# The end of a mixture-of-experts kernel: one branch instead of two, last sums of different banks declared independent, and idle products moved ahead of them

## The chip, the cores and the metric

The kernel runs on one core of a Trainium2 chip. The core has five engines that run side by side, each with its own queue of instructions: TensorE (PE: matrix products, and PEld: its weight loads), VectorE (DVE), ScalarE (ACT), GpSimd (POOL) and SyncE (SP, which here issues most of the transfers). [...] Time is device time in microseconds (us); lower is better. Three runs of the kernel before took 394.36, 396.98 and 397.94 us, median 396.98.

## What is computed

One transformer block on 16 sequences of 256 tokens of width 128, all in float32. It has causal attention with 16 heads of width 8, and eight experts of inner width 512, of which each token uses the two with the highest router logits. Layer norm comes after each half:

```python
def reference(x, w_qkv, w_proj, b_proj, W_router, b_router, W1, b1, W2, b2):
    x = _layernorm(x + attention(x, w_qkv, w_proj, b_proj))
    logits = x @ W_router + b_router
    top_vals, top_idx = jax.lax.top_k(logits, 2)
    weights = softmax over the two chosen logits
    y = sum over experts e of weights[:, e] * (relu(x @ W1[e] + b1[e]) @ W2[e] + b2[e])
    return _layernorm(x + y)
```

## The kernel before, in words

The program has a main path (`main_path`), which is quick and holds for ordinary data, and a plain `general_path` that recomputes everything. A flag, `spoiled`, says whether the main path met a softmax denominator outside a safe range; at the very end every engine loads that flag and skips the general path if it is zero (L1621, L1622).

The main path works in this order. Attention is done for one sequence ("batch") after the other. After batches 0 to 9, and again after 10 to 15, the tokens are routed: this makes two groups, group 0 of ten batches and group 1 of six. Tokens are scattered to DRAM, sorted by expert (`route`, L1046; `finish`, L1181, ends with the tables of block starts and a flag in `over` for more blocks than planned). Blocks of 128 or 256 rows of one expert are then fetched, put through both layers, and sent back to DRAM at the tokens' places (`block`, L1289). If a group had more blocks than planned, `leftover` (L1579) would do up to two more per group: it stands behind a first branch on the flag `any_over`, taken by every engine (L1580, L1581).

At the end of each group, `combine` (L1420) goes over its batches. For each batch: `fetch` (SyncE) loads the two experts' results of each token, tile `ys`; `add` sums them with the residual; `stats` (VectorE, `moments_of`, L742) takes mean and variance; `power` (GpSimd) raises the variance to −1/2; `shift` (VectorE) makes the offset; `scale` (ScalarE) writes the result to `yout`, of which there are three buffers; SyncE stores it.

In the last group `add` is done by TensorE, as products with the identity that accumulate in PSUM (L1465); `begin` (L1443) has put the residual there earlier. [...] Batches 0 to 3 of the last group use the four banks of one tile, `room`, a bank each; batches 4 and 5 have tiles of their own, of the kind "m", which has three buffers that go round. Because `room` is one tile, the framework that sets the semaphores makes an `add` into one bank wait for earlier reads of another bank of it.

`keep_warm` (L1538) makes twelve idle products whose result nobody reads. `check` (L1551) has `within` (VectorE: counts the good denominators), `total` (TensorE: one product that adds the counts over partitions), `missing` (VectorE: writes `spoiled`) and `exceeded` (VectorE: writes `any_over`).

The order of the work is written out: every step is registered as an operation with a number, a planner's cost and a rank, but `emit` only follows the list `ORDER` (L311). Costs, ranks and port flags of the operations are not read when the list is there. The list fixes each engine's own order; what waits for what between engines follows from the data. In it, five idle products stand while the last blocks run and seven after everything else. The last sums come in the order of batches 2, 4, 5, 3, 1, 0.

Of the kernel before, what the change touches and what calls it, by code (L numbers as in the profile page):

```python
# [22 lines left out]
HEADS = 16  # L23
# [318 lines left out]
499 782 610 611 612 530 531 932 933 892 500 783 784 980 981 645 1541 785 767 982 934 935 769  # L342
# [6 lines left out]
878 818 819 1227 848 891 820 1020 821 822 849 1021 1032 823 890 850 1018 877 939 824 1033 1542  # L349
1198 1034 949 1035 940 1543 1036 851 1494 1022 852 941 942 1023 948 1024 1235 950 968 951 943  # L350
1025 826 825 1231 944 969 1026 952 970 1229 1236 945 946 953 971 972 1037 1237 1048 1049 1205
954 973 906 955 1050 1051 1544 905 1201 956 974 975 1200 1027 907 908 976 947 1052 1053 909 911
1199 1088 910 912 1008 1054 913 1089 1090 914 959 915 1091 1055 957 977 960 958 961 1056 988
1092 1093 962 1094 963 1009 1095 1096 964 965 1210 1217 1216 966 989 1010 916 990 1011 1012
1057 918 917 919 991 801 802 1013 992 1097 853 1496 1014 1015 993 994 1219 1221 995 1016 920
921 922 967 996 923 803 998 854 1068 1069 1017 997 1222 804 805 807 806 808 924 925 926 855 856
809 999 810 811 858 1070 860 1078 857 1071 1079 859 1072 1073 861 1213 1212 927 1000 862 1074
1001 1002 863 1080 1211 1493 827 1075 1076 813 812 1003 828 1081 1082 1004 1005 1215 1038 1039
1083 829 830 1084 864 865 1085 1098 831 1006 1040 832 833 1041 1042 1077 834 1058 1043 1059 835
1060 1044 1061 1086 1099 836 1100 1062 1214 1007 1220 1045 1101 837 1102 1218 1063 1046 1251  # L360
1103 1064 1065 1087 1104 1393 1252 1253 1066 1105 1254 1255 839 838 1394 1047 1395 1256 1106
1257 1258 1483 1067 1264 1107 1484 1278 1277 1265 1172 1156 1396 1397 1398 1259 1260 1261 1485
1486 1399 1400 1401 1140 1279 1280 1173 1164 1487 1488 1282 1281 1263 1174 1262 1374 1284 1266
1373 1283 1267 1489 1175 1490 1402 1108 1141 1491 1353 1176 1177 1142 1132 1269 1354 1285 1286
1375 1376 1492 1268 1271 1178 1377 1143 1179 1287 1270 1144 1145 1378 1239 1157 1238 1158 1333
1146 1272 1289 1273 1159 1274 1288 1334 1355 1356 1160 1148 1363 1379 1240 1276 1357 1275 1343
1241 1380 1161 1133 1242 1381 1364 1358 1244 1243 1382 1290 1134 1135 1245 1162 1335 1336 1136
1344 1147 1359 1360 1361 1137 1149 1362 1291 1180 1337 1246 1338 1313 1247 1248 1250 1365 1366
1314 1249 1138 1150 1339 1340 1367 1345 1346 1347 1341 1342 1423 1163 1463 1368 1292 1151 1165
1293 1348 1166 1369 1370 1371 1167 1294 1296 1295 1372 1424 1297 1315 1316 1152 1153 1168 1169  # L370
1139 1349 1350 1464 1154 1124 1109 1323 1317 1318 1351 1324 1298 1299 1425 1170 1352 1300 1426
1413 1110 1319 1465 1466 1155 1320 1301 1427 1302 1111 1428 1321 1467 1414 1181 1325 1326 1429
1322 1468 1430 1431 1327 1433 1434 1469 1182 1432 1328 1470 1471 1415 1112 1329 1416 1417 1330
1435 1331 1418 1453 1183 1436 1437 1438 1472 1304 1419 1420 1421 1303 1454 1113 1332 1305 1473
1404 1403 1114 1439 1306 1440 1441 1422 1455 1307 1456 1457 1308 1474 1458 1442 1184 1185 1186
1405 1406 1309 1310 1407 1475 1408 1476 1459 1443 1444 1311 1384 1383 1312 1477 1460 1478 1461
1462 1445 1446 1409 1410 1411 1116 1412 1187 1447 1448 1385 1386 1479 1480 1387 1481 1449 1388
1125 1389 1450 1545 1546 1390 1482 1117 1451 1497 1118 1452 1391 1119 1115 1547 1392 1548 1126
1127 1128 1120 1129 1549 1121 1171 1498 1495 1513 1514 1515 1516 1122 1527 1528 1529 1130 1530
1517 1518 1534 1535 1536 1537 1520 1123 1506 1521 1531 1522 1532 1131 1538 1539 1507 1508 1523  # L380
1499 1500 1524 1501 1519 1533 1540 1509 1510 1525 1526 1511 1502 1503 1504 1512 1505 1550 1551
1552 1553 1554 1555 1556
# [72 lines left out]
def main_path(  # L455
# [64 lines left out]
    plans = [Plan()]  # L520
    plans[0].banks = {"sc", "ps_o", "m"}
    bufs = {p1: 1, p2: 2, p3: 3, p4: 4, p6: 6, p8: 8, ps_sc: 1, ps_o: 1, ps_m: 3}

    def op(*a, **kw):
        return plans[-1].op(*a, **kw)

    def tile_of(pool, tag, shape, dtype=F32):
        return plans[-1].tile(pool, shape, tag, bufs[pool], dtype)
# [61 lines left out]
    any_over = const.tile([1, 1], I32, name="any_over")  # L590
# [151 lines left out]
    def moments_of(mv, r):  # L742
        st = p4.tile([P, 6], F32, tag="st", name="st")
        V.bn_stats(st, r)  # L744
        V.bn_aggr(mv, st)

# [299 lines left out]
    def route(g, b, n):  # L1046
# [106 lines left out]
        chosen = op("DVE", 1.05, z, logits, after=[*x1_ops[b : b + n], br_op, table_op])  # L1153
        chosen = op("DVE", 1.15, z, choose, after=[chosen])
        chosen = op("DVE", 1.9, z, choose_next, after=[chosen])
        mats(z, 0.48, count, writes=[psc], after=[chosen])
        a = op("ACT", 0.12, z, weights_exp, after=[chosen])
        weighted = op("DVE", 0.6, z, weights, after=[a])
        g.placed = op("DVE", 1.8, z, totals, reads=[psc], after=counted)
        g.placed = op("DVE", 0.72, z, places, after=[g.placed])  # L1160
# [20 lines left out]
    def finish(g):  # L1181
# [90 lines left out]
        for k, n, fn, cost in ((1, g.ND, pairs, 1.65), (0, g.NB, singles, 1.6)):  # L1272
            experts, starts = of_each(n, str(k))
            go = op("DVE", cost, z, fn, after=[go])
            go = g.ready[k] = op("DVE", 0.45 + 0.015 * n, z, experts, after=[go])
            go = g.known[k] = op("DVE", 1.1 + 0.02 * n, z, starts, after=[go])
# [143 lines left out]
    def combine(g, sent):  # L1420
# [8 lines left out]
        acc, room = [], tile_of(ps_sc, "sc", [P, GROUPS, 2, S])  # L1429
        for b in range(g.n):  # L1430
            if not last:
                acc.append(tile_of(p2, "acc", [P, NT, D]))
            elif b < GROUPS:
                acc.append(tile_of(ps_sc, f"acc{b}", []))
                acc[b].get = lambda b=b: room.get()[:, b].rearrange(
                    "p a (o d) -> p (a o) d", d=D
                )[:, 0:NT, :]
            else:
                acc.append(tile_of(ps_m, "m", [P, NT, D]))

            def begin(b=b):
                rows = x1_sb[:, rows_of(b), 0:D]
                nc.tensor.matmul(  # L1443
                    acc[b].get(), ident, rows, start=True, stop=False, skip_group_check=True
                )

            if last:
                where, after = ([room], x1_ops) if b < GROUPS else ([], g.second)
                mats(z0 + 6.0 * b, 0.43, begin, writes=[*where, acc[b]], after=after, part="begin")

        for b in range(g.n):
# [9 lines left out]
            def add(b=b, ys=ys):  # L1461
                a = acc[b].get()
                if last:
                    for k in range(2):
                        nc.tensor.matmul(  # L1465
                            a,
                            ident,
                            ys.get()[:, :, k],
                            start=False,
                            stop=k == 1,  # L1470
                            skip_group_check=True,
                        )
                else:
# [3 lines left out]
            def stats(b=b, mv=mv):  # L1477
                for n in range(NT):
                    moments_of(mv.get()[:, n, :], acc[b].get()[:, n, :])
# [10 lines left out]
            def scale(b=b, rstd=rstd, off=off, yout=yout):  # L1490
                for n in range(NT):
                    nc.scalar.activation(
# [5 lines left out]
                    )  # L1498

            op("SP", 0.5, z, fetch, kb=256, writes=[ys], after=sent)  # L1500
            if last:
                mats(z, 0.88, add, reads=[ys], writes=[acc[b]])
# [35 lines left out]
    def keep_warm():  # L1538
        g = groups[-1]
# [7 lines left out]
        for i in range(WARM):  # L1547
            mats(2900.0, 0.43, turn_over, writes=[idle], after=g.second)


    def check():  # L1551
# [13 lines left out]
        def missing():  # L1565
            V.tensor_scalar(spoiled, psg.get(), -1.0, float(B * HEADS * S), ALU.mult, ALU.add)

        def exceeded():
            with nc.allow_low_precision(reason="0 or 1"):
                V.tensor_reduce(any_over, over, AX.X, ALU.max)  # L1570

        go = op("DVE", 2.6, z, within, writes=[good], after=dens_ops)
        mats(z, 0.2, total, writes=[psg], after=[go])
        op("DVE", 0.16, z, missing, reads=[psg])
        op("DVE", 0.16, 10.0 * B + 100.0, exceeded, after=found)

    def leftover():  # L1579
        some = nc.values_load(any_over[0:1, 0:1])  # L1580
        with tc.If(some > 0):  # L1581
            plans.append(Plan())
            for g in groups:
                sent = []
                for j in range(g.NB - SPARE, g.NB):
                    sent += block(g, j, 0)
                combine(g, sent)
            for o in plans[-1].ops:
                o["fn"]()
# [5 lines left out]
    b0, groups = 0, []  # L1595
    for r, chunks in enumerate(ROUTED):
# [9 lines left out]
        combine(g, sent)  # L1606
        groups.append(g)
    check()
    keep_warm()
    nc.scalar.preload_act_table_set("natural_log_exp_and_others")  # L1610
    with tc.manual_schedule():
        plans[0].emit()
    leftover()
# [68 lines left out]
```

## Time and profile before

The profile is of one execution that took 396.12 us by the device's own measure; from its first to its last instruction (the span) are 394.3 us.

| what | value |
|---|---|
| runs | 394.36, 396.98, 397.94 us; median 396.98 |
| profiled execution, span | 396.12 us, 394.3 us |
| mean granted TensorE clock | 0.962 |
| TensorE products / weight loads busy | 340.9 us (86%) / 250.5 us (64%) |
| VectorE, ScalarE, GpSimd busy | 212.5, 253.2, 218.7 us (54, 64, 55%) |
| from 0 to 370 us | attention, routing, experts, group 0's end |
| 370 to 387 us | group 1's end: products busy 11.63 us, statistics and scaling |
| 387 to 394.3 us | no engine is busy; branches and the end of the program |
| last sum (batch 0) | starts 382.53, on "sc" |
| last scaling (ScalarE) | ends 386.87 |
| last store | issued 386.89 |

How to read it. Engines are named as above; a name ending in q (DVEq, SPq) is the engine's sequencer, which does branches, flag loads and waits and is not counted as busy. "L1465" is a line of the kernel. In a group such as "sc<-ys,ident" the tile on the left is written from those on the right: "sc" is the tile `room`. An idle stretch is put down to what ended it, after "<-". The chain of waits is followed back from the last instruction of an engine; "issue" in it is time in which the engine waited for nothing that the profile shows. The windows view gives, for a stretch, its length, each engine's busy time, the granted clock of TensorE, the DMA engines' mean busy share and what they moved.

### The profile page before, as it was taken

Reading aid. Unit: us, or ns where it says so; the run is one execution under the profiler, and the core shown is the slowest. Engines: PE = TensorE matmul, PEld = TensorE weight load, DVE = VectorE, ACT = ScalarE, POOL = GpSimd, SP = SyncE. Lnnn points to the kernel's source line nnn. Section 1 sums busy time; section 2 is a strip of 40 time slices with the busy share of each in tenths; the row PEclk is TensorE's granted clock in tenths of the full one; section 3 lists DMA queues with packets and bytes.
Section 4 is the critical chain, followed back from the end, with each engine's and each line's share of the span. In section 5 each row is a group of like instructions: output and inputs, shape, how many; then the busy total and the mean of one; then the engine's idle time right before and its main releaser. Section 6 shows DMA issues by size and latency. Waiting matters only on the chain.

```text
span 394.3 us, 9755 instructions
## 1 busy us (share of the span) xinstructions
PE 340.9 (86%) x2960; PEld 250.5 (64%) x2960; DVE 212.5 (54%) x730; ACT 253.2 (64%) x547; POOL 218.7 (55%) x252
## 2 busy tenths in 40 slices
PE   5999999589986789759899899989899999999672
PEld 4555555256542455335479779878899898889651
DVE  3434457956778578794557872432222376633450
ACT  2788888368868277736645545555576688877522
POOL 5335434437886386867623367777776445454340
PEclk9999999979999699978999989999999999999988
DMA  5201322013241141343424635566755777766341
GB/s 134 17 4 45 95 76 56 23 52 91 73 129 30 37 115 58 83 120 89 134 62 140 159 123 142 154 191 173 209 155 163 240 226 226 212 190 191 110 148 51
DMA packets 53104, 46.57 MB, mean 118 GB/s; under 512 B 14610, under 2 KB 39577, under 8 KB 53042
## 3 DMA queue, kind: packets, MB, share of 16 engines
q1 hardware_dynamic: 48626, 37.36, 35.3%
q0 software_dynamic: 4416, 8.47, 6.4%
q8 instruction: 28, 0.46, 0.5%
q14 instruction: 34, 0.28, 0.2%
HBM read 33.53 MB, written 12.67 MB: 117 GB/s over the span
## 4 chain that ended last, share of the span: by engine, by line
PE 58%; DVE 18%; ACT 9%; DMA 8%; issue 4%; ACTq 0%; SPq 0%; DVEq 0%; POOLq 0%; POOL 0%
PE m L1337 14%; PE m L1358 14%; PE sc L869 9%; PE ps_o L910 8%; ACT pr L894 5%; PE m L791 5%; DMA spread<-recs 4%; PE m L964 2%; DVE key L1066 2%; DMA w<-in_L_ffn_W_dram 2%; DVE x_sb L994 1%; PE m L836 1%; DVE st L744 1%; PE sc L1465 1%; PE m L1321 1%
## 5 line engine op out<-in xcount | busy, mean ns | idle before, releaser
L1385 POOL DMA_INDIRECT back<-yw,rows_in x74 | 73.5, 993 | 62.8 <-ACT yw L1377 39.8
L894 ACT ACTIVATE pr<-sc 128x2048 f32<-128x2048 f32 x48 | 90.1, 1877 | 25.7 <-PE sc L869 25.0
L879 POOL TENSOR_SCALAR_AFFINE_SELECT pr<-pr 128x1024 f32<-128x1024 f32 (+1 forms) x48 | 68.5, 1435 | 65.0 <-ACT pr L894 60.4
L1350 ACT ACTIVATE hT<-m,b_sb 128x128 f32<-128x128 f32 (+1 forms) x224 | 72.1, 405 | 27.5 <-PE m L1337 19.1
L1337 PE MATMUL m<-rT,w 128*128 128x128 f32 (+1 forms) x448 | 75.9, 316 | 4.8 <-DVE rT L1330 3.0
L1138 POOL DMA_INDIRECT rows<-x_sb,dest x64 | 64.1, 1002 | 27.9 <-issue 17.1
L1358 PE MATMUL m<-w_sb,hT 128*128 x592 | 76.1, 278 | 2.4 <-ACT hT L1350 1.4
L1358 PEld LDWEIGHTS m<-w_sb,hT 128*128 128x128 f32 x592 | 71.3, 191 | 5.2 <-ACT hT L1350 3.6
L1337 PEld LDWEIGHTS m<-rT,w 128*128 128x128 f32 x448 | 62.3, 192 | 12.7 <-DVE rT L1330 5.2
L869 PE MATMUL sc<-qTm,qk 32*128 32x512 f32 x384 | 56.2, 655 | 7.9 <-ACT pr L894 7.2
L910 PE MATMUL ps_o<-pr,va 128*32 128x128 f32 (+1 forms) x1024 | 51.2, 342 | 0.5 <-ACT o L923 0.4
L1368 DVE TENSOR_TENSOR y<-m,b_sb 128x128 f32<-128x128 f32 (+1 forms) x56 | 18.7, 334 | 61.0 <-PE m L1358 39.3
L1377 ACT ACTIVATE yw<-y,rows_in 128x128 f32<-128x128 f32 x74 | 27.6, 400 | 30.0 <-DVE y L1368 27.5
L910 PEld LDWEIGHTS ps_o<-pr,va 128*32 128x32 f32 x1024 | 29.5, 115 | 22.5 <-issue 9.0
L820 ACT ACTIVATE qTm<-qk,rows_sb 128x256 f32<-128x256 f32 x64 | 29.8, 503 | 5.3 <-DVE qk L808 5.3
L869 PEld LDWEIGHTS sc<-qTm,qk 32*128 32x128 f32 x384 | 15.6, 190 | 21.7 <-ACT pr L894 18.1
L791 PE MATMUL m<-xT,wqk_sb 128*128 128x256 f32 x64 | 22.8, 440 | 5.3 <-ACT xT L781 5.3
L954 DVE TENSOR_TENSOR o<-o,spread 128x512 f32<-128x512 f32 x16 | 16.2, 1015 | 15.0 <-DMA spread<-recs 15.0
L791 PEld LDWEIGHTS m<-xT,wqk_sb 128*128 128x128 f32 x64 | 11.1, 206 | 19.6 <-ACT xT L781 8.1
L800 DVE TENSOR_TENSOR part<-m,rope_sb 128x256 f32<-128x256 f32 x32 | 13.2, 411 | 19.3 <-PE m L791 19.2
L964 PEld LDWEIGHTS m<-wproj_sb,o 128*128 128x128 f32 x128 | 16.1, 190 | 10.1 <-DVE o L954 4.5
L964 PE MATMUL m<-wproj_sb,o 128*128 128x136 f32 x128 | 18.5, 288 | 2.3 <-DVE o L954 2.1
(151 smaller groups left out, 377.7 us busy)
## 6 DMA issues: line engine op xcount, KB each, us to landing
w<-in_L_ffn_W_dram SPq DMA_DIRECT2D x56, 256.0 KB
spread<-recs SPq DMA_DIRECT2D x16, 256.0 KB
ys<-back SPq DMA_DIRECT2D x16, 256.0 KB
rows_in<-rows SPq DMA_DIRECT2D x38, 65.0 KB
rows_in<-rows SPq DMA_DIRECT2D x18, 130.0 KB
x<-in_L_attn_x_dram SPq DMA_DIRECT2D x16, 128.0 KB
w_sb<-in_L_ffn_W_dram SPq DMA_DIRECT2D x8, 256.0 KB
out_dram<-yout SPq DMA_DIRECT2D x16, 128.0 KB
```

The lines of the kernel that those rows point to most:

```text
L791: nc.tensor.matmul(ps.get()[:, c, :], w[:, s, :], xT.get(), start=True, stop=True)
L820: lambda j=j: nc.scalar.activation(qTm.get()[:, j, :], qk.get()[:, 0], AF.Copy, scale=rows_sb[:, j : j + 1]),
L869: nc.tensor.matmul(ps.get()[:, g], qk.get()[rg, 1, ts(kt, P)], qTm.get()[rg, js, kt * P : S], start=True, stop=True,)
L879: nc.gpsimd.affine_select(out=pr.get()[:, :, :, 0:P], in_=pr.get()[:, :, :, 0:P], compare_op=ALU.is_ge, fill=0.0, base=0, pattern=[[0, GRO ...
L894: lambda pr=pr, ps=ps: nc.scalar.activation(pr.get(), ps.get(), AF.Exp),
L910: nc.tensor.matmul(pso.get()[ts(g, 32), t, kt * P : S], va_t[:, kt, 2 * g + t].rearrange("p u c -> p (u c)")[:, 16 * u : 16 * u + 32], pr. ...
L964: nc.tensor.matmul(ps_p.get()[:, q, :], o.get()[:, t, ts(q, P)], wproj_sb[:, t, :], start=(t == 0), stop=(t == 1),)
L1138: nc.gpsimd.indirect_dma_start(out=g.rows[:, :], out_offset=bass.IndirectOffsetOnAxis(ap=g.dest[:, k, t - g.t0 : t - g.t0 + 1], axis=0), i ...
L1337: nc.tensor.matmul(ps_h[i].get()[:, c, :], w.get()[:, ts(i * per + c, P)], rT.get()[:, 0 : n * P], start=True, stop=True,)
L1350: nc.scalar.activation(hT.get()[:, at, 0 : n * P], ps_h[i].get()[:, c, :], AF.Relu, bias=bias)
L1358: nc.tensor.matmul(ps_y.get()[:, i, :], hT.get()[:, c, i * P : (i + 1) * P], w2_sb[:, bass.ds(e, 1), c, :].rearrange("p o d -> p (o d)"), ...
L1385: put = nc.gpsimd.indirect_dma_start(out=g.back[:, :], out_offset=bass.IndirectOffsetOnAxis(ap=rows_in.get()[:, i, D : D + 1].bitcast(I32) ...
```

## The change

Four things are done.

1. **One branch.** `leftover` and its branch go. `missing` now adds "a group had more blocks than planned" to the flag `spoiled`, so that one branch at the end serves both cases: such data go to the general path. `exceeded` goes as an operation of its own; the three small steps are one operation.
2. **The check is moved** in the order: `total` and `missing` stood apart in the expert stage of group 0, `exceeded` later; now `total` and `missing` stand directly behind the last operation of `finish` of group 1.
3. **Independence.** A helper `apart` collects the instructions that touch the banks of `room` in the last `combine`, and declares any two of them that are on different engines and on different banks free of a dependency.
4. **Idle products.** `keep_warm` is registered ahead of the last `combine`, its products are prerequisites of the sums, and in the order the seven that stood at the very end now stand between `begin` of batch 2 and the sum of batch 2.

Beside that the fetches of the last group stand earlier in the list, all before the first sum. Each engine's own order, SyncE's transfers included, is otherwise as before. The operations' numbers change, since the idle products are registered earlier and one operation less exists; so nearly all lines of `ORDER` differ, and they are left out here.

```diff
-    any_over = const.tile([1, 1], I32, name="any_over")
+    any_over = const.tile([1, 1], F32, name="any_over")
+    lost = const.tile([1, 1], F32, name="lost")
...
     def moments_of(mv, r):
         st = p4.tile([P, 6], F32, tag="st", name="st")
-        V.bn_stats(st, r)
+        read = V.bn_stats(st, r)
         V.bn_aggr(mv, st)
+        return read
...
-    def combine(g, sent):
+    def combine(g, sent, warm=()):
...
+        used_by = []
+
+        def apart(b, engine, put):
+            if last and b < GROUPS:
+                for other, by, i in used_by:
+                    if other != b and by != engine:
+                        tc.declare_no_dep(put.ins, i.ins, reason="another bank")
+                used_by.append((b, engine, put))
...
-                nc.tensor.matmul(
+                put = nc.tensor.matmul(
                     acc[b].get(), ident, rows, start=True, stop=False, skip_group_check=True
                 )
+                apart(b, PE, put)
...
-                        nc.tensor.matmul(
+                        put = nc.tensor.matmul(
                             a,
                             ident,
                             ys.get()[:, :, k],
...
+                        apart(b, PE, put)
...
-                    moments_of(mv.get()[:, n, :], acc[b].get()[:, n, :])
+                    apart(b, DVE, moments_of(mv.get()[:, n, :], acc[b].get()[:, n, :]))
...
-                    nc.scalar.activation(
+                    read = nc.scalar.activation(
                         yout.get()[:, n, :],
...
+                    apart(b, ACT, read)
...
-                mats(z, 0.88, add, reads=[ys], writes=[acc[b]])
+                mats(z, 0.88, add, reads=[ys], writes=[acc[b]], after=warm)
...
-        for i in range(WARM):
-            mats(2900.0, 0.43, turn_over, writes=[idle], after=g.second)
+        return [mats(2900.0, 0.43, turn_over, writes=[idle], after=g.second) for _ in range(WARM)]
...
         def missing():
-            V.tensor_scalar(spoiled, psg.get(), -1.0, float(B * HEADS * S), ALU.mult, ALU.add)
-
-        def exceeded():
-            with nc.allow_low_precision(reason="0 or 1"):
-                V.tensor_reduce(any_over, over, AX.X, ALU.max)
+            V.tensor_scalar(lost, psg.get(), -1.0, float(B * HEADS * S), ALU.mult, ALU.add)
+            V.tensor_reduce(any_over, over, AX.X, ALU.max)
+            V.tensor_tensor(spoiled, lost, any_over, ALU.add)
...
-        mats(z, 0.2, total, writes=[psg], after=[go])
-        op("DVE", 0.16, z, missing, reads=[psg])
-        op("DVE", 0.16, 10.0 * B + 100.0, exceeded, after=found)
-
-    def leftover():
-        some = nc.values_load(any_over[0:1, 0:1])
-        with tc.If(some > 0):
...
+        mats(z, 0.2, total, writes=[psg], after=[go, *found])
+        op("DVE", 0.55, z, missing, reads=[psg], after=found, port=True)
...
-        combine(g, sent)
-        groups.append(g)
+        combine(g, sent, keep_warm(g) if g.r == len(ROUTED) - 1 else [])
     check()
-    keep_warm()
     nc.scalar.preload_act_table_set("natural_log_exp_and_others")
     with tc.manual_schedule():
-        plans[0].emit()
-    leftover()
+        plan.emit()
```

The planner's costs and port flags of the routing steps change too (L1153 to L1160 and L1272 to L1276).

## The prediction

> **What bounds the kernel now.** I read the page's slices first: TensorE is busy in nearly every slice until the last one or two, where nothing is at its limit. The change touches only the end and one small check, so I went to the chain of waits from 369 us on. Columns: start, length, what. "sc" and "m" are PSUM tiles; L1465 is the last sums, L1492 the final scaling.
>
> ```profile
> 371.00 2.62 DMA ys<-back
> 373.67 1.30 PE sc L1465 x4
> 374.97 1.72 PE m L1465 x4
> 376.69 1.07 issue
> 377.76 0.82 ACT yout L1492 x2
> 378.57 0.04 issue
> 378.62 1.15 PE sc L1465 x4
> ...
> 380.61 1.15 PE sc L1465 x4
> ...
> 382.53 1.15 PE sc L1465 x4
> ```
>
> The six last sums are those of batches 2, 4, 5, 3, 1, 0 in that order. The sum of batch 3 starts 0.04 us after ScalarE has scaled batch 2; those of 1 and 0 start 0.04 us after statistics of 3 and 1. These are different banks of one tile ("room"): a step of 1.9 us per batch that the data do not ask for. The windows view, cut where the clock changes (PE, PEld, DVE, ACT, POOL busy, then granted clock, DMA share, GB/s):
>
> ```profile
> 371.10:374.50 3.40, 0.83 (x4) 0.76 (x5) 0.69 (x6) 1.65 (x4) 0.00 (x0) 1.00 0.74 224
> 374.50:377.90 3.40, 3.40 (x10) 2.36 (x8) 1.74 (x9) 0.14 (x1) 1.14 (x3) 0.50 0.92 290
> ```
>
> After 3.4 us with TensorE mostly idle the next 3.4 us run at half clock, and the sums of batches 4 and 5 fall there: 1.9 us each instead of 1.15. Last, the two branches: L1580 and L1581 are the first, L1621 and L1622 the second, L1677 the program's end. Columns: line, engine queue, instruction, count, ns, start of the first and last.
>
> ```profile
> L1581 DVEq EVENT_SEMAPHORE  x2: 21/21/21, 389.4 to 389.5; - x2
> ...
> L1581 DVEq COMPARE_BRANCH  x1: 72/72/72, 386.2 to 386.2; - x1
> ```
>
> ```profile
> L1622 DVEq COMPARE_BRANCH  x1: 56/56/56, 390.0 to 390.0; - x1
> ...
> L1622 DVEq EVENT_SEMAPHORE  x1: 21/21/21, 393.2 to 393.2; - x1
> ```
>
> And what SyncE's queue waited for at the very end:
>
> ```profile
> SPq L1677 <- DVEq L1622: 0.9, 1, 0.9
> ```
>
> VectorE's sequencer needs 3.2 us from each branch to its next instruction, twice in a row, and the last thing SyncE waits for is that second jump. The span ends 7.4 us after the last scaling (386.87 to 394.3).
>
> [...] SyncE's second jump took 1.35 (389.9 to 391.3). [...]
>
> **The change, part by part.** Durations are of the one profiled execution: span 394.3, its own time 396.12.
>
> *Idle products.* Seven of twelve move from behind the sums to ahead of them, behind the start of batch 2's bank (issued 370.06 and 370.28). Each is two matmul records; fourteen took 3.18 us in the tail, 0.216 apart. From 370.49 they occupy 14 x 0.216 = 3.02 us, to 373.51, under the 2.62 us wait for the fetch "ys", which lands at 373.62. So they cost nothing; their cover is 0.1 us, and if the fetch came earlier they would hold the first sum by as much. Gain: [...] sums 2, 4 and 5 run at 1.13–1.15 us. At half clock instead the fourteen would end at 376.5, which is a rival below.
>
> *Independence of banks.* Removes the waits of sums 3, 1, 0. What is late next is the landing of the fetches. The trace's landing records (last of 16 marks each) give batches 2, 4, 5, 3, 1, 0: 373.63, 374.30, 376.29, 376.92, 377.92, 378.96; SyncE's order of transfers is unchanged, so I keep these. Sums then end at 374.80, 375.66, 377.46, 378.3, 379.2, 380.1. Behind them is a chain of VectorE statistics (0.91 per batch, 375.01 to 375.92), GpSimd power (1.02, 376.01 to 377.03), VectorE shift (0.13), ScalarE scale (0.82), with hops of 0.03 to 0.1. VectorE keeps its order: statistics 2, 4, shift 2, statistics 5, shift 4, and so on. Statistics then end: batch 2 375.74, 4 376.65, 5 378.40 (waits for the fetch), 3 379.43, 1 380.61, 0 381.65. Powers end 376.85, 377.89, 379.51, 380.55, 381.72, 382.76. Shift 0 starts 382.80, scale 0 runs 383.03 to 383.85, against 386.05 to 386.87: **3.0 us less**. Output buffers: the sixth scaling needs the third's store landed; it would be issued at 380.55 and the same store took 1.81 (381.82 to 383.63), so lands 382.4, 0.6 before it is needed.
>
> *One branch.* Removed per engine: a load of the flag (0.28 to 0.57), a compare, a jump, and SyncE's nine marks. VectorE: the load starts with the last shift and the branch comes 0.40 later, 383.20, plus 3.25 for the jump = 386.45. SyncE: last store issued 383.87, landed 2.36 later as before (386.89 to 389.25), 386.23; its own load, branch and 1.35 jump are through at 386.0, so the landing decides. Then 4 marks at 0.067, 12 checks at 0.062 and the closing handshake, 0.84 (393.46 to 394.30): 386.23 + 0.27 + 0.74 + 0.84 = **388.1**. VectorE is 0.6 us early. So from the last scaling to the end 4.25 instead of 7.4: **3.15 us less**. PE (3.58 us jump) starts its jump by 380 and is not late; GpSimd's drain of 2.68 would end near 386.6. If SyncE's single jump took VectorE's 3.2 instead of 1.35, add 1.6; if its first jump's 0.49 (387.65 to 388.14), nothing, since the landing decides.
>
> *The check.* `total` and `missing` move behind the last routing step, which ends at 258.91; `exceeded` (0.13, at 261.44) joins them, and one new 1x1 addition (0.14 like its neighbours). On PE the 0.19 us product comes before the second layer at 258.59, and PE then waits 1.1 us for rows until 260.86: hidden. On VectorE `missing` adds a wait for `total`, issued about 258.6, so none in fact; some 0.5 us of work fits into its gap until 259.80. Queued behind it is that bias addition, and ScalarE's weighing waits for it: without the gap, 0.5 us. The bank of `total` moves in the rotation of three: at 251.4 one wait of 0.2 us on it goes, at 258.6 it needs the bank freed at 258.47 by the same activation that the next product needs. Bounds −0.2 to +0.8, taken as 0. The planner's new costs and port flags are not read, since the order is written out; order and SyncE queue are otherwise the same on each engine.
>
> Sum: 3.0 + 3.15 = 6.15, span 394.3 − 6.15 = 388.15; with the 1.8 us around it 389.95 for this execution. The median of the runs shown, 396.98, lies 0.86 above it, so I forecast 396.98 − 6.15 = **390.8**.
>
> **Rivals.**
> 1. *The bank waits stay, or another wait takes their place* (output buffers, GpSimd's pace): only the clock helps. Then scale 2 starts at 377.1 instead of 377.76 and the chain shifts by 0.7: 396.98 − 0.7 − 3.15 = 393.1. For it: the power step, 1.02, is nearly the pace already, and the buffers have 0.6 us. Against: all three waits named are between banks that the new declarations name.
> 2. *The products start late or at half clock, or the jump is dear.* Products to 376.5 put every sum 2.9 later; less the 0.7 that was lost to batch 5's fetch, the tail gains 0.85: 393.0. A dear SyncE jump alone: 392.4. Against: the clock was 1.00 from 364 to 374.5.
> 3. *Slower.* One mechanism: the expert stage from 259 to 365 is shifted a little by the check and meets its weight fetches later. The chain shows one wait of 3.76 us for a weight at 354.65. Each further one costs as much; it decides from two (7.5 over 6.15): 398.3. For: DMA share 0.68 there. Against: SyncE's order is the same and the shift is under 0.8 us.
>
> **How the numbers follow.** Chances: forecast 0.68, rival 1 0.14, rival 2 0.10, rival 3 0.04, and 0.04 for more gain than worked out ([...] stores landing in 1.8). Single runs of before spread from 394.36 to 397.94, so ±1.8 around 390.8 is the forecast's own width; rivals 1 and 2 lie at 392.4 to 393.1. Range 388.8 to 393.4: below it most of the larger gain, above it rival 3 and the upper part of rival 1. Within 1% of 396.98, which is about what a measurement can tell from no change, is 393.0 to 400.95: half of rival 1, a third of rival 2, most of rival 3 and the forecast's tail, 0.16. Slower by over 1%: 0.02. Faster: 0.82.
>
> **What would show it.** Right: granted clock 1.00 through 374.5 to 378; no sum waiting for a scaling or for statistics; sums of batches 5, 3, 1, 0 waiting for their fetches; one VectorE jump of 3.2 us; span about 388. Wrong: L1465 still released by L1492 or L744; ScalarE waiting for a store; SyncE's last wait over 1 us on an engine; the first sum starting later than 373.8; a span that already differs by over 1 us at the end of the expert stage (about 368.5).

## The result, and the profile after

The kernel after took 393.49 us (median of 4 runs, 390.35 to 395.17), the kernel before in the same session 397.46 (4 runs, 394.36 to 399.03): ratio 0.990, interval 0.985 to 0.995. That is faster, as forecast, by about 1%; whether it is more than the 1% that the prediction called hardly to be told from no change stays open. As it stands, 393.49 lies 0.1 us above the predicted range (388.8 to 393.4) and 2.7 above the point forecast of 390.8. But the range was set from a base of 396.98, and a fourth run of the kernel before (399.03) raised that base to 397.46; the ratio on the old base gives 392.9, inside the range and 2.1 above the forecast. Ratios, here and below, come from fast runs alone (within 1.5% of the kernel's fastest) and medians from all runs, so that the two need not agree, and the profiled executions of e2 and e6 were slow ones.

The profiled execution took 393.34 us, span 391.6, against 396.12 and 394.3. Cut at two marks, the spans show where the difference lies. The marks are the issue of the last group's first fetch of `ys`, and the end of the last scaling. All times are us:

| | before | after | predicted for after |
|---|---|---|---|
| start to first fetch | 371.00 | 374.19 | 371.0 |
| first fetch to end of last scaling | 15.86 | 12.88 | 12.85 |
| end of last scaling to end of span | 7.47 | 4.57 | 4.25 |
| the last two together | 23.34 | 17.45 | 17.1 |

So the tail, which the change is about, became 5.9 us shorter, of the 6.15 that were forecast. In this execution 3.2 us were lost again ahead of it. The experiments go after both.

The chain of waits of the kernel after, from the idle products on (start, length, what; L1557 is the idle product, L1478 the last sum, L1506 the final scaling):

```profile
373.95 3.02 PE ps_o L1557 x14
376.97 1.11 PE sc L1478 x4
...
379.43 0.74 POOL rstd L1497
...
382.74 0.81 ACT yout L1506 x2
383.56 0.02 issue
383.57 2.58 DMA out_dram<-yout
...
386.26 0.34 ACT yout L1506
386.60 0.02 issue
386.62 0.45 ACT yout L1506
```

The two waits between banks (a sum released by a scaling, then by statistics) are gone from the chain. The fourteen product records take 3.02 us as worked out and end 0.07 after the first fetch has landed (376.90; a transfer has landed with the last of the 16 marks that the trace records for it), so they cost nearly nothing. But the chain now ends on something that was not in it: a *store* of 2.58 us, ahead of the last scaling. The waits view of the same kernel, 374 to 390 us (total, times, longest), shows what each engine stood for:

```profile
DVE off L1500 <- POOL rstd L1497: 1.6, 4, 0.8
PEld sc L1478 <- DMA ys<-back: 0.9, 3, 0.4
...
ACT yout L1506 <- DMA out_dram<-yout: 0.5, 1, 0.5
```

The sums wait for fetches, VectorE for GpSimd's power, and ScalarE once, 0.5 us, for an output buffer. The windows view, cut as before:

```profile
371.10:374.50 3.40, 3.40 (x18) 2.99 (x17) 2.53 (x14) 1.16 (x5) 1.44 (x2) 1.00 0.12 39
374.50:377.90 3.40, 3.40 (x16) 2.70 (x15) 0.58 (x5) 1.65 (x4) 0.00 (x0) 1.00 0.76 209
377.90:381.30 3.40, 3.21 (x15) 2.30 (x14) 2.68 (x15) 0.81 (x2) 1.87 (x4) 1.00 0.97 318
```

TensorE (first number) is busy throughout, and the clock (1.00) holds where it was 0.50. Last the branch, L1615, of which there is one (line, queue, instruction, count, ns, start of first and last):

```profile
L1615 PEldq COMPARE_BRANCH  x1: 3769/3769/3769, 382.7 to 382.7; - x1
...
L1615 DVEq COMPARE_BRANCH  x1: 72/72/72, 386.1 to 386.1; - x1
...
L1615 DVEq EVENT_SEMAPHORE  x1: 21/21/21, 389.4 to 389.4; - x1
```

VectorE needs 3.3 us from its branch to its next instruction, once. SyncE's own waits from 384 to 392 us include these two:

```profile
SPq L1615 <- SPq L1615: 1.6, 2, 1.2
...
SPq L1670 <- PEq L1670: 0.7, 2, 0.5
```

The second is the closing handshake, which stood there before with the same 0.7. The 0.9 us that SyncE had waited for VectorE's second jump is gone.

Of the runs below, e1 to e4 were made on a chip whose granted clock was lower and wandered (0.91 to 0.95, against 0.95 to 0.98 elsewhere), where the kernel before takes about 449 us. Runs e5 to e8 come from a second chip and e9 to e12 from a third, both with the kernel before at about 398 us.

### The profile page after: what moved, and what is told of

Read it like the earlier page. It is cut to its first block, busy times and chain, and to the rows that moved or that the text cites. A ratio compares the mean times of both kernels' runs of the same rounds, so it can differ in the third digit from the quotient of the medians.

```text
span 391.6 us, 9729 instructions
## 1 busy us (share of the span) xinstructions
PE 340.1 (87%) x2960; PEld 250.1 (64%) x2960; DVE 213.1 (54%) x731; ACT 253.5 (65%) x547; POOL 218.2 (56%) x252
## 4 chain that ended last, share of the span: by engine, by line
PE 59%; DVE 18%; ACT 10%; DMA 6%; issue 3%; SPq 1%; POOL 0%; ACTq 0%; DVEq 0%
PE m L1360 14%; PE m L1339 13%; PE sc L871 10%; PE ps_o L912 8%; ACT pr L896 6%; PE m L793 5%; PE m L966 3%; DVE key L1068 2%; PE m L838 2%; DMA rows_in<-rows 1%; DMA spread<-recs 1%; PE ps_o L1557 1%; DVE x_sb L996 1%; DMA ys<-back 1%; DVE st L745 1%
## 5 line engine op out<-in xcount | busy, mean ns | idle before, releaser
L1360 PE MATMUL m<-w_sb,hT 128*128 x592 | 76.7, 279 | 3.5 <-ACT hT L1352 1.5
L1360 PEld LDWEIGHTS m<-w_sb,hT 128*128 128x128 f32 x592 | 71.3, 191 | 7.3 <-ACT hT L1352 3.6
L1339 PEld LDWEIGHTS m<-rT,w 128*128 128x128 f32 x448 | 63.1, 195 | 11.5 <-DVE rT L1332 5.1
L793 PE MATMUL m<-xT,wsw_sb 128*128 128x256 f32 x64 | 20.4, 403 | 0.0
```

What stands on the lines that cost most here:

```text
L793: nc.tensor.matmul(ps.get()[:, c, :], w[:, s, :], xT.get(), start=True, stop=True)
L1339: nc.tensor.matmul(ps_h[i].get()[:, c, :], w.get()[:, ts(i * per + c, P)], rT.get()[:, 0 : n * P], start=True, stop=True,)
L1360: nc.tensor.matmul(ps_y.get()[:, i, :], hT.get()[:, c, i * P : (i + 1) * P], w2_sb[:, bass.ds(e, 1), c, :].rearrange("p o d -> p (o d)"), ...
```

## The experiments

The theory was: the forecast's mechanism is right, its gain is all in the tail, and what is missing in the time is drift in the expert stage that the change does not cause. Its rivals were that the moved check delays the expert stage, and that the jump which is left costs more at the end than the forecast allowed. The kernel before was run beside each. The ratios of the first four tell little about 5 us, so three of these kernels were repeated on the third chip (e9, e10, e11).

Result of all (medians; ratio to before with its 95% interval; then the segments of each profile, named as above, us):

| run | median | before | ratio | to fetch | fetch to scaling end | to end |
|---|---|---|---|---|---|---|
| e1_whole | 445.85 | 449.36 | 0.993 [0.990, 0.996] | 425.59 | 13.98 | 4.65 |
| e2_tail_only | 447.76 | 449.36 | 1.002 [0.998, 1.005] | 428.56 | 14.25 | 6.48 |
| e3_branch_only | 448.66 | 449.36 | 1.008 [1.004, 1.012] | 419.08 | 16.43 | 5.41 |
| e4_check_place | 450.69 | 449.36 | 1.004 [1.001, 1.008] | 423.94 | 16.97 | 7.43 |
| e5_banks_tied | 394.42 | 397.69 | 0.994 [0.991, 0.997] | 373.33 | 15.26 | 5.37 |
| e6_products_last | 393.24 | 397.69 | 0.988 [0.985, 0.992] | 375.22 | 14.59 | 4.35 |
| e7_no_branch | 388.91 | 397.69 | 0.976 [0.971, 0.981] | 371.02 | 12.99 | 3.02 |
| e8_fourth_buffer | 392.49 | 397.69 | 0.988 [0.982, 0.995] | 370.44 | 12.62 | 4.80 |
| e9_whole_again | 393.42 | 398.12 | 0.989 [0.986, 0.993] | 372.68 | 13.01 | 4.38 |
| e10_tail_again | 396.18 | 398.12 | 0.995 [0.992, 0.997] | 373.67 | 14.75 | 6.60 |
| e11_branch_again | 394.77 | 398.12 | 0.991 [0.988, 0.994] | 373.39 | 15.84 | 5.29 |
| e12_short_body | 390.13 | 398.12 | 0.982 [0.976, 0.988] | 372.69 | 12.37 | 3.08 |

**The whole change, twice.** The kernel after, unaltered.

> The whole change once more, with more rounds. Theory D (drift): the tail and the end give about 6 us, and the 3.2 us by which the expert stage ended later in the first profile (fetch of the last group issued at 374.2 instead of 371.0) are chance of the transfers: the ratio comes out at 0.984 to 0.987, and in this profile the fetch is issued anywhere from 370 to 375. Theory C (caused): the new place of the check, or the shorter program, makes the expert stage 2 to 3 us later in every run: ratio 0.989 to 0.993, fetch at 373 or later. From the fetch to the end both expect 17.4 us, against 23.3 before.

> The whole change a third time, to set it beside its two halves on one chip. Theory D (what was lost ahead of the last group's fetch is chance): ratio 0.983 to 0.988, fetch to end 17.2 to 17.8 us. Theory C (a loss of 2 us or more in the expert stage that comes with the change): 0.989 to 0.993.

The two executions nearly repeat the tail of the first profile: 13.98 and 13.01 to the last scaling, 4.65 and 4.38 from there. e9 puts the whole change at 4.7 us (398.12 to 393.42). The first profile's lost 3.2 us before the tail did not come again in full: e9's first fetch is issued at 372.68, between the 371.00 of before and 374.19. The ratios, 0.993 and 0.989, both missed what drift was to give (at most 0.987 and 0.988) and lie in the ranges of the rival, a loss that comes with the change.

**The tail alone**, twice: the kernel before with the independence of banks, and with the idle products and fetches in their new order; two branches and the old check stay.

```diff
+        def apart(b, engine, put):
+            if last and b < GROUPS:
...
-                nc.tensor.matmul(
+                put = nc.tensor.matmul(
...
+                apart(b, PE, put)
```

> Before with only the independence of banks and the idle products moved; two branches and the check as before. Theory D: ratio 0.991 to 0.994 (3.0 us off), from fetch to end 20.2 to 20.5 us. Theory C: the same gain, and the fetch at 371 as in before, since the check stands in its old place. A third, that the gain of the sums is lost again in the two branches: ratio over 0.997.

> Only the independence of banks and the idle products moved. Theory D: the gain of the tail by itself, 3.0 to 3.7 us: ratio 0.990 to 0.993, fetch to last scaling 12.6 to 13.2 us. Theory C with the check as its cause: the same. If the tail's gain is only a matter of profiled executions: ratio 0.996 or more.

**The branch alone**, twice: the kernel after with `apart` switched off and the order of the tail as before.

```diff
-            if last and b < GROUPS:
+            if False and last and b < GROUPS:
...
-                mats(z, 0.88, add, reads=[ys], writes=[acc[b]], after=warm)
+                mats(z, 0.88, add, reads=[ys], writes=[acc[b]])
```

> Before with only the one branch and the merged check in its new place; last sums and idle products as before. Theory D: ratio 0.991 to 0.994 (3.15 us off), from fetch to end about 20.2 us. Theory C: the loss in the expert stage eats most of it: ratio 0.997 to 1.001, fetch at 373 or later.

> Only the one branch, with the check in its new place. Theory D: ratio 0.991 to 0.995 (2.0 to 3.2 us off), last scaling to end 4.4 to 5.5 us. Theory C: the check's place takes it back, ratio 0.997 to 1.002.

On the third chip the means of all runs fall by 1.9 (tail) and 3.5 us (branch), 5.4 together, against 4.7 for the whole. Only the branch's ratio, 0.991, came out as expected; the tail's, 0.995, lies between the expected and the rival's. The branch alone keeps the old tail to the last scaling (15.84 against 15.86) and takes 2.2 us off behind it. The tail alone takes 0.9 us off behind the last scaling, but only 1.1 us off ahead of it instead of 3.0, which I had not foreseen. Its chain of waits says why:

```profile
382.69 0.81 ACT yout L1503 x2
383.50 0.02 issue
383.52 3.98 DMA out_dram<-yout
...
387.61 0.33 ACT yout L1503
```

The third store took 3.98 us there, and the sixth scaling, which takes over its buffer, waited 1.9 us for it. Ahead of this wait the 3.0 us are there: the last shift ends 12.0 us after the fetch, against 15.0 in before. With two branches still there, TensorE's stand at 382.32 and 383.72, and transfers of 16 KB that the profile calls "instruction" start at 383.67 and 384.92, while that store is under way (more on this below). The ratios on the first chip can't decide between the halves: the tail alone has 1.002, and the branch alone 1.008, though its median lies 0.7 below that of before and the same kernel has 0.991 in e11.

**The check's place.** The kernel before with `total`, `missing` and `exceeded` (1542, 1543, 1544 in its `ORDER`) put behind the last routing step (1237), and nothing else.

```diff
-... 824 1033 1542
-1198 1034 949 1035 940 1543 1036 ...
-... 973 906 955 1050 1051 1544 905 ...
+... 972 1037 1237 1542 1543 1544 1048 ...
```

> Before with only the check's three steps moved behind the last routing step, as the change has them; two branches, sums as before. Theory D: no difference, ratio 0.997 to 1.003. Theory C, if the check's place is the cause: ratio 1.005 to 1.008, and the stage from 259 us to the fetch 2 to 3 us longer.

Its ratio, 1.004, lies between what the theory (up to 1.003) and the rival (from 1.005) expected, and leans against the new place; the medians differ by 1.3 us in 449. Its fetch, at 423.94, lies among those of that chip's three other kernels (419.08 to 428.56), which spread too far to show where 1.3 us should have gone. In the profile after, VectorE's timeline about the check reads (start, busy, line, operation, then the idle time before and what ended it):

```profile
258.71 0.15 DVE L1579 TENSOR_SCALAR lost<-m 1x1 f32<-1x1 f32 x1
258.79 0.13 DVE L1580 TENSOR_REDUCE any_over<-over 1x1 f32<-1x2 f32 x1
258.95 0.15 DVE L1581 TENSOR_TENSOR spoiled<-lost,any_over 1x1 int32<-1x1 f32 x1
260.17 0.29 DVE L1370 TENSOR_TENSOR y<-m,b_sb 128x128 f32<-128x128 f32 x1 [1.07 <-PE m L1360]
```

After the three steps VectorE stands idle for 1.07 us, so for VectorE itself there is room. But what it waits for is TensorE, and TensorE had waited 0.33 us for the check (put down to L1580). In before the same addition (L1368 there) came sooner:

```profile
259.80 0.29 DVE L1368 TENSOR_TENSOR y<-m,b_sb 128x128 f32<-128x128 f32 x1 [0.89 <-PE m L1358]
```

The chain of waits of e9, the whole change again, goes right through the check (L1576 is `total`, L1360 the block's second layer):

```profile
258.79 0.13 PE m L1576 x2
...
258.95 0.15 DVE lost L1579
259.09 0.07 DVE any_over L1580
...
259.24 1.14 PE m L1360 x8
```

From the end of the block's first layer to this addition, the profiles of before and e10 take 0.93 us and e2 1.25; all eleven with the check in its new place take 1.61 to 1.80. So the new place puts about 0.7 us into that block every time. In the first profile it is hidden, since TensorE then waits for the next rows in any case; in e9 it is not. That is a cost that comes with the change, though a small one. What ties TensorE's product to these steps, the bank that `total` uses or something else, was not tried.

**Banks tied again.** The kernel after with `apart` switched off (the first two lines of the last diff), products ahead as in the change.

> The whole change without the declarations of independence. From the fetch of the last group to the end of the last scaling the whole change took 12.9 us (first chip) and 14.0 (second). Theory: the sums of batches 3, 1, 0 wait again for the reads of another bank, only 0.7 us earlier than before: 2.0 to 2.5 us more than the whole change on the same chip. Rival: the pace of GpSimd's power and of the fetches would have set the same times anyway: 0 to 0.4 more.

The last scaling comes 15.26 after the fetch, against 12.88: the independence is worth 2.4 us there, in line with the steps that it removes. The waits view has the old waits back, sums behind statistics, with the figures of before (its line stands first):

```profile
PEld sc L1465 <- DVE st L744: 2.5, 2, 1.3
```

```profile
PEld sc L1478 <- DVE st L745: 2.5, 2, 1.3
```

Its time, 394.42, is 1.0 above that of e9, which ran on another chip, and the intervals of the two ratios overlap; the segment carries this reading, the median only agrees in sign.

**Products last.** The kernel after with the seven products at the very end of the order and not asked for ahead of the sums.

```diff
-                mats(z, 0.88, add, reads=[ys], writes=[acc[b]], after=warm)
+                mats(z, 0.88, add, reads=[ys], writes=[acc[b]])
```

> The whole change with the seven idle products back at the very end. Theory: the clock halves for 3.4 us while sums 4 and 5 run, statistics of batch 5 start 0.8 later, and fetch to last scaling takes 0.6 to 1.0 us more than the whole change. Rival: with the banks independent the landings and GpSimd's power hide it: under 0.3 more.

Its windows show the half clock again:

```profile
374.90:378.30 3.40, 0.29 (x1) 0.29 (x2) 1.02 (x8) 1.65 (x4) 0.00 (x0) 1.00 0.57 167
378.30:381.70 3.40, 3.40 (x9) 2.59 (x9) 0.96 (x5) 0.00 (x0) 0.73 (x2) 0.50 0.98 302
```

The stretch with TensorE busy for 0.29 of 3.40 us was followed by one with the clock at 0.50, in which the sums fall; the last scaling comes 14.59 after the fetch, 1.7 later than in the profile after, more than the 0.6 to 1.0 that I had expected. Not all of that is the clock: ScalarE waits 1.3 us for a store here (0.5 there), and the third fetch lands 5.8 us after the first one's issue (4.9 there). A cleaner pair is e11 and e5, both with the banks tied and neither with a wait for a store: 15.84 with the products last, 15.26 with them ahead, 0.6 us. The time of e6, 393.24, shows nothing of it. So the half clock behind the idle stretch is shown, but what the products are worth beside independent banks is not.

**No branch at all.** The kernel after without its last lines. It leaves out the fallback to the general path.

```diff
-    bad = tc.nc.values_load(spoiled[0:1, 0:1])
-    with tc.If(bad > 0):
-        general_path(tc, *args)
```

> The whole change without the last branch too; it leaves out that the general path runs where the flag says so, and nothing else. Theory: the landing of the last store decides the end, so that the branch that is left costs little: from last scaling to end 4.2 to 4.6 us, as in the whole change (4.6). Rival: the jump that is left is still the bound (VectorE's 3.2 us or SyncE's): 1.5 to 3 us less.

From the last scaling to the end 3.02 us instead of 4.57: the branch that is left still costs 1.55 us at the end, and its ratio (0.976) is clear of the whole change's. My expectation, 4.2 to 4.6, was wrong. The rival's figure, 1.5 to 3 us less, just holds, though VectorE's jump is not what ends last (389.37, the store's last mark 389.66). Half of the 1.55 is the last store's landing, 0.75 us sooner after its issue; the other 0.80 lies behind the landing (1.18 us to the end instead of 1.98), where SyncE with a branch still has five marks and twelve checks to go through, and without one five checks. All six stores land in 1.81 to 1.83 us here. In the profile after they take 1.84, 1.83, 2.58, 2.21, 1.82 and 2.56. The transfers view of both, from 378 to 388.2 us (queue, kind, packets, MB, share of 16 engines), first of the kernel after:

```profile
q8 instruction: 2, 0.03, 1.1%
q14 instruction: 2, 0.02, 0.5%
```

Without the branch there is no such line, only that of the data:

```profile
q1 hardware_dynamic: 1664, 0.82, 25.9%
```

What the view calls "instruction" the trace's records show singly, but neither for which engine nor what released it. In the profile after a 16 KB one starts at 384.05 (TensorE's branch was at 382.66) while the third store, issued 383.57, is under way; another starts at 387.10, 1.0 us after VectorE's branch and with the issue of the last store. They took 0.88 and 0.90 us. Those two stores took 2.58 and 2.56 us, and only one or two of their 16 marks came late: in the third, fifteen stood 1.80 us after the issue; in the last, fourteen 1.84. The kernel without the branch has no such transfer before its end.

**A fourth output buffer.** If the wait for the buffer is the harm, one more buffer ends it.

```diff
-            ys, yout = tile_of(p6, "ys", [P, NT, 2, D]), tile_of(p3, "yout", [P, NT, D])
+            ys, yout = tile_of(p6, "ys", [P, NT, 2, D]), tile_of(p4, "yout", [P, NT, D])
```

> The whole change with four output buffers in place of three. In the profile of the change the last scaling waits 0.6 us for a store of batch 5 that took 2.6 us to land. Theory: fetch to last scaling 0.5 to 0.7 us shorter where a store is that slow, 0 where stores land in 1.8. Rival: the last shift is no earlier and the wait only moves to the store's own landing: no difference.

It did not end it. With four buffers the sixth scaling takes over the *second* one's, and that store was slow this time, as its chain says:

```profile
378.47 3.68 DMA out_dram<-yout
...
382.26 0.33 ACT yout L1506
```

ScalarE waited 0.4 us. The last scaling comes 0.3 sooner after the fetch, less than expected where a store is slow, and the median (392.49) can't be told from the whole change's.

**A short body.** The kernel after with a body that only writes one word. It leaves out the general path's recomputation.

```diff
     with tc.If(bad > 0):
-        general_path(tc, *args)
+        tc.nc.vector.memset(spoiled, 0)
```

> The whole change with the branch kept, but a single tiny instruction behind it in place of the general path, so that the place jumped to lies close; it leaves out the recomputation where the flag would ask for it. In the whole change the last store took 2.56 us to land, without any branch 1.81. Theory: [...] with a short jump the store lands in 1.75 to 1.9 us and last scaling to end is 3.6 to 3.9 us instead of 4.6; VectorE goes on within 1 us of its branch instead of 3.2. Rival: the later landing comes from the flag's loads or the marks, not from the jump's length: landing 2.4 or more, end 4.4 or more.

The framework put this small branch where the flag is ready, not at the end, so the run is not the "short jump at the end" that I meant, and what it was to decide stays undecided. What it does show:

```profile
L1615 DVEq COMPARE_BRANCH  x1: 72/72/72, 269.4 to 269.4; - x1
...
L1615 DVEq EVENT_SEMAPHORE  x1: 21/21/21, 269.7 to 269.7; - x1
```

A jump over this one instruction takes VectorE 0.2 us (269.44 to 269.67), where the one over the general path takes 3.3. At the end there is no jump and no "instruction" transfer, all stores take 1.81 to 1.83, and the last 3.08 us are like those of no branch at all.

## Why the prediction was right, and where it was not

**Idle products: right.** They cost nearly nothing (they end 0.07 us behind the first fetch), and the clock is 1.00 where it was 0.50. What went before is in the windows: TensorE busy for 3.40 of 3.40 us in after, for 0.83 in before. Without the products ahead, 0.29 us busy were followed by 0.50 again (e6). The price of the half clock is 0.6 us with the banks tied (e11 and e5) and not separated from store and fetch with the banks independent.

**Independence of banks: right in mechanism and sum.** Last scaling 12.88 after the fetch, predicted 12.85. Different banks of `room` are in use at once: TensorE's last three sums run on it from 380.09 to 383.13, while ScalarE reads batch 2 from it from 380.44 to 381.25. But two errors cancel in it. The chain of fetches, statistics and powers was 0.4 quicker: the shift of batch 0 starts 11.39 after the fetch, predicted 11.80, since the landings came up to 0.4 sooner. The step "the same store took 1.81 ..., so lands 0.6 before it is needed" was mis-sized: it took 2.58. At 1.81 it would have landed at 385.38, some 0.4 before ScalarE could use it; it landed at 386.16 and ScalarE waited 0.5 (1.4 in e1, 1.0 in e9). I had named this wait as a sign of being wrong, and as part of the first rival. It is there, but it takes 0.5 to 1.4 us and not the 2.3 which that rival needed.

**One branch: right but for 0.3 us.** 4.57 against 4.25: the last store landed 2.56 after issue (2.36 assumed), and landing to end took 1.98 (1.85). That the landing decides and VectorE is early holds: its jump ends at 389.37, the store's last mark comes at 389.66. What I missed is that the landing differs with and without the jump. Before's last two stores (2.77 and 2.36) had "instruction" transfers beside them too, four of 8 KB and one of 16 KB that start between 387.4 and 388.7, and I carried 2.36 over as a property of the last store. Without a jump it is 1.81 (e7). The halves show the same: taking the tail's 3.0 us with two jumps at the end gives 1.1 (e10), where the third store took 3.98 with two 16 KB transfers beside it and ScalarE waited 1.9 for it. In the segments the halves give 2.0 and 2.2 us, 4.2 together, against 5.9 for the whole. The means (5.4 against 4.7) don't show this: they carry an error of about 0.5 us each.

Slow stores, jumps and "instruction" transfers go together: with the jump at the end some stores of every profile take 2.1 to 4.0 us, without it (two kernels) all twelve take 1.81 to 1.83. Store by store it is sharper. Of the 84 stores of the last group in all 14 profiles, 39 have an "instruction" transfer beside their first 1.3 us (a mark set after the count was made) and take 1.92 to 3.98 us; the other 45 take 1.81 to 1.89. No run kept the jump and took away the transfer alone, so that the transfers are what held up the stores was not shown, nor what brings them on.

**The check: taken as 0, and not 0.** It is within its bounds (−0.2 to +0.8), but the step "PE then waits 1.1 us for rows until 260.86: hidden" took the slack of one execution for a property of the kernel, and the working had no wait of TensorE for VectorE's three steps. The traces show that wait and 0.7 us in the block; where the rows are there in time, as in e9, it stands on the chain. The timing of the check alone, e4, leans the same way by 0.4%.

**Base and noise: the larger part of the miss.** "396.98 − 6.15" assumes that the start of the tail stays. In the first profile it came 3.2 us later, one of the signs of being wrong that the prediction named. The trace places that between 316 and 356 us. SyncE's transfers were later (one wait of 3.2 us for `back` against 0.9 in before), TensorE was busy for 1.38 of the 3.40 us from 349.5, and it then ran at half clock (0.50) for 3.4 us; in before there is no half clock between the routing and the tail.

Is it caused? Take the mean time of each kernel, less its profile's fetch-to-end and the 1.7 us around the span, as an estimate of its usual fetch: before 372.0 to 373.0 by session, e10 (old check) 373.1; with the new check e5 372.4, e6 372.8, e7 371.0, e8 373.5, e9 374.2, e11 371.8, e12 373.2, the kernel after 374.0. The mean of these eight is 372.9. So this estimate shows no loss common to the new check or branch, which was the third rival. The profiles lean the other way: from the end of the routing (about 259 us) to the fetch, before and e10 take 112.1 and 112.7 us, the eight with the new check 112.9 to 115.4; up to the routing's end they are no later (257.2 to 260.6, against 258.9 and 261.0). Two profiles with the old place are too few to size this, but a loss of about 1 us, of which the check's 0.7 would be a part, is not ruled out. On the first chip the same stage shows no order (136.4 us with the old place; 131.6, 135.7 and 138.8 with the new).

Beside that the profiles scatter by 3 us or more, though the kernels do the same work up to there. Part of it goes with the clock: e7, e8 and e9 have 17.1 us of half clock ahead of the fetch, which comes at 370.4 to 372.7; e6 has 30.7 us, and its fetch comes at 375.2. The other six have 20.5 to 23.9 us, and fetches at 371.0 to 374.2. Before's profiled execution, fetch at 371.00, was 1 to 2 us early against its usual one.

What stays open: by their means the whole change brings 4.0 (first session), 3.9 (e1) and 4.7 us (e9), its tail 5.9 in the profiles. It falls short by 1.2 to 2.0 us all three times. The check can explain up to 0.7 of that; for the rest I have only the scatter of the expert stage to point to, and its cause is not settled; nor is why e7 gains 8.8, 1.5 more than its own segments (23.34 − 16.01 = 7.3) explain.

## What to carry to other kernels

Work out a tail by landings and chains as here, but give a store that may run beside a jump a range and not the duration of the row above: here 1.81 us without a jump (e7), up to 3.98 with "instruction" transfers beside it (e10). A gap that hides a new step in one profile may be absent in the next execution: follow what waits for the new step, on every engine, before it is priced at 0. Before adding gains of two edits at one end, ask whether one edit's work now falls into the other's transfers. And when an edit takes a few us off the last 25, compare the segments first: the medians here moved by 2 to 3 us between kernels for reasons ahead of the edit.

## What the runs showed of the hardware

- The jump over the general path took VectorE 3.0 to 3.9 us until its next instruction (before 3.25, after 3.29) and TensorE 3.3 to 4.1 (3.64, 3.83), but SyncE 0.4 to 1.35 (1.35, 0.49) and GpSimd 0.2 to 0.5 (0.49, 0.22). Over `leftover` VectorE took 2.9 to 3.2 too (before 3.18), TensorE 0.4 (before 0.37). A jump over one instruction took each of them 0.2 to 0.3 (e12).
- "Instruction" transfers at these jumps, 16 KB in 0.9 to 1.6 us (before 1.10 and 1.24, after 0.88 and 0.90), went with slower 128 KB stores under way: 3.98 us instead of 1.83 in the worst case (e10).
- The 128 KB stores with no "instruction" transfer beside their first 1.3 us landed 1.81 to 1.89 us after their issue (45 stores in 14 profiles).
- A stretch of 3.4 us with TensorE busy for 0.29 (e6), 0.83 (before) or 1.38 us (after, from 349.5) was followed by one with a granted clock of 0.50.
